# Column-tiled transposes and spreads, and score matmuls of 64 keys, in a transformer block

## The chip, the core and the metric

The kernel runs on one core of a Trainium2 chip. The metric is the device time of one execution in microseconds (us). The engines are PE (TensorE, matmuls; PEld are its weight loads), DVE (VectorE), ACT (ScalarE), POOL (GpSimd) and SP (SyncE, which only issues DMAs here).

## What is computed

One transformer block with conditioned norms, for x of 4 x 1024 x 512, 16 heads of 32 channels, a hidden width of 2048, all in float32:

```python
def _tc_rmsnorm(x, t, gw, gb, bw, bb):
    g = (t @ gw.T + gb)[:, None, :]
    b = (t @ bw.T + bb)[:, None, :]
    inv_rms = jax.lax.rsqrt(jnp.mean(x * x, axis=-1, keepdims=True) + EPS)
    return g * x * inv_rms + b

def _attention(x, Wq, Wk, Wv, Wo):
    ...
    attn = jnp.einsum('blhd,bmhd->bhlm', q, k) / scale
    p = jax.nn.softmax(attn, axis=-1)
    o = jnp.einsum('bhlm,bmhd->blhd', p, v).reshape(B, L, D)
    return o @ Wo.T

def _swiglu(x, gate_w, hid_w, out_w):
    return jax.nn.silu(x @ gate_w.T) * (x @ hid_w.T) @ out_w.T
...
x1 = x + _attention(_tc_rmsnorm(x, t, g1...), Wq, Wk, Wv, Wo)
x2 = x1 + _swiglu(_tc_rmsnorm(x1, t, g2...), gate_w, hid_w, out_w)
return x + x2
```

The softmax subtracts each row's maximum before the exponential.

## The kernel before

**Layout.** Channels lie on the 128 partitions and tokens along the free axis. The tokens come in 8 blocks of 512 (two for each of the 4 batch entries). Heads are taken in 4 groups of `HG` = 4 heads (4 x 32 = 128 channels), queries in runs of `HQ` = 256, keys in units of 256 (`UN` = 4 units for 1024 keys).

**Steps.** One main loop runs over `g`. Step g computes the raw scores of one unit: 4 heads, 256 queries, 256 keys, so there are 256 such steps; four steps (the kinds g mod 4 = 0 to 3, as counted by `kind`) cover one head group and one run of queries, a group of four steps. The later parts of that attention work follow a few steps behind. From `FS` = 60 on, the feed-forward part of an earlier block is woven into the same steps (`pair_15`, `pair_26`, `pair_7`, `pair_3`, `pair_4`, `contract`: the tiles `pa`, `pb` and `pc`); before it, the projections of queries, keys and values (`pkq`, `pv`) are. After the last scores only feed-forward work is left. The order of the instructions on PE, DVE, ACT and POOL is written out by hand in this loop; each engine runs its own list in order and waits on semaphores.

**Tilings of PE's array.** A matmul with weights of K rows and M columns may use a part of the array: with 32 rows and 128 columns four matmuls of different rows can be in the array, with 128 rows and 32 columns four of different columns. `mm` (line 103) cuts a matmul into column pieces of `columns[0]`, which the loop sets to 32 at the top of each step and to 128 for a while in steps of kind 0 before g = 60. So feed-forward and projection blocks are mostly tiled 128x32, as is `weighted` (line 368, tile `av`: the probabilities times the values, one matmul for each key block and head into that head's 32 partitions). Each float32 matmul call becomes two pairs of a weight load and a matmul instruction; a bfloat16 call becomes one pair.

**The parts that the change touches.**

- `scores` (line 301, matmul on line 310, tile `sc`): for each of two blocks of 128 keys and each of the four heads, one matmul whose weights are that head's 32 rows of 128 keys and whose moving operand is that head's 32 rows of 256 queries. 8 calls a step, tiled 32x128. `keep` (line 315) copies `sc` to `raw` on ACT, with one buffer of `sc`.
- `running_max`, `max_T` and `parts` (lines 319 to 342): DVE takes the maximum over the key blocks, PE transposes it (tile `mt`) and DVE writes the negative of the maximum as three bfloat16 numbers that add up to it, for each head, into columns 0 to 11 (`NP` = 12) of `split`. The remaining columns are zeros.
- `parts_T` (line 344, transposes on line 347, tile `pt`): in steps of kind 1, two bfloat16 transposes of the whole 128x128 `split`, and a copy of the first 12 rows to `mT` on ACT (line 349).
- `spread` (line 351, matmul on line 357, tile `sp`): called twice in steps of kind 1, each time for two of the four heads. A matmul of `select` (12 rows, 128 columns of zeros and ones for each head) with `mT` adds the three parts of the head's negative maximum and spreads the sum over all 128 partitions; ACT copies that to `shift` (line 358). 2 calls each time.
- `shifted` (line 360, DVE) adds `shift` to `raw`, `exponential` (line 365, ACT) takes the exponential in place, and `weighted` and `accumulate` (a DMA issued by POOL) use it.

In a step of kind 1 the order on PE is `parts_T`, `scores`, `spread` of the first two heads, `weighted`, `spread` of the other two, and then the feed-forward or projection blocks:

```python
            if kind == 1 and m_on:
                parts_T(j_m)
            if g < NR:
                scores(g)
            if kind == 1 and m_on:
                spread(j_m, 0)
...
            if v_on:
                weighted(r_v)
                accumulate(r_v)
            if kind == 1 and m_on:
                spread(j_m, 2)
```

In the other steps it is `scores`, `weighted`, then the rest. In the feed-forward stage `weighted` and the feed-forward blocks around it are tiled 128x32.

Of the kernel before, what the change touches and what calls it, by code (L numbers as in the profile page):

```python
# [11 lines left out]
BF16 = mybir.dt.bfloat16  # L12
# [5 lines left out]
P = 128  # L18
# [6 lines left out]
def tile_cond_transformer_block(  # L25
# [13 lines left out]
    nc = tc.nc  # L39
# [7 lines left out]
    DH = D // N_HEADS  # L47
    HG = P // DH
    FG = 4
    HQ = 256  # L50
# [6 lines left out]
    const = ctx.enter_context(tc.tile_pool(name="const", bufs=1))  # L57
    sb = ctx.enter_context(tc.tile_pool(name="sb", bufs=1))
# [8 lines left out]
    ident_bf = const.tile([P, P], BF16, tag="ident_bf", name="ident_bf")  # L67
# [8 lines left out]
    NP = 3 * HG  # L76
    split = [const.tile([P, QT, P], BF16, tag=f"split{i}", name=f"split{i}") for i in range(2)]
# [2 lines left out]

    pick = const.tile([NP, HG], F32, tag="pick", name="pick")
    nc.vector.tensor_reduce(pick, ident[:NP, :NP].rearrange("p (h i) -> p h i", i=3), AX.X, ALU.add)
    select = const.tile([NP, HG, P], BF16, tag="select", name="select")
    nc.vector.tensor_copy(select, pick.unsqueeze(2).to_broadcast([NP, HG, P]))
    mod = const.tile([P, 4 * C, B], F32, tag="mod", name="mod")

    condT = const.tile([P, B], F32, tag="condT", name="condT")
# [15 lines left out]
    def mm(dst, w, moving, start: bool, stop: bool, seeded: bool = False):  # L103
        n = columns[0]
        for k in range(0, P, n):
            nc.tensor.matmul(  # L106
                dst[k : k + n, :], w[:, k : k + n], moving, start=start, stop=stop, skip_group_check=seeded
            )

    y, wkq, wv, wo, kq, v = {}, {}, {}, {}, {}, {}  # L110
    raw, rmax, shift, mT, av, acc, avs, oT = {}, {}, {}, {}, {}, {}, {}, {}
# [189 lines left out]
    def scores(r: int):  # L301

        j, u = divmod(r, UN)
        m, qh = divmod(j, NB // HQ)
        keys, queries = kq[m, 0, u], kq[m, 1, qh]
        sc = ps_sc.tile([P, HG, 2, HQ], F32, tag="sc", name=f"sc{r}")
        for k in range(2):
            for i in range(HG):
                rows = slice(i * DH, (i + 1) * DH)
                nc.tensor.matmul(  # L310
                    sc[:, i, k, :], keys[rows, k * P : (k + 1) * P], queries[rows, :], start=True, stop=True
                )
        state["sc", r] = sc

    def keep(r: int):
# [28 lines left out]
    def parts_T(j: int):  # L344
        pt = ps.tile([P, HQ // P, P], BF16, tag="w", name=f"pt{j}")
        for qt in range(HQ // P):
            nc.tensor.transpose(pt[:, qt, :], split[j % 2][:, qt, :], ident_bf)
        mT[j] = sb.tile([NP, HQ], BF16, tag="mT", name=f"mT{j}", bufs=2)
        nc.scalar.copy(mT[j], pt[:NP, :, :].rearrange("p a b -> p (a b)"))

    def spread(j: int, k: int):

        if k == 0:
            shift[j] = sb.tile([P, HG, HQ], F32, tag="shift", name=f"shift{j}")
        pp = ps.tile([P, 2, HQ], F32, tag="w", name=f"sp{j}_{k}")
        for i in range(2):
            nc.tensor.matmul(pp[:, i, :], select[:, k + i, :], mT[j], start=True, stop=True)
        nc.scalar.copy(shift[j][:, k : k + 2, :], pp)  # L358

    def shifted(r: int, heads: slice = slice(0, HG)):  # L360
# [262 lines left out]
    for b in range(1, B):  # L623
        for half in range(QB):
            s = math.ceil((len(queue) + 1) / PACE)
            s4 = s - 4 - (s - 6) % UN
            tag = f"a{b}_{half}"
# [14 lines left out]
    for n in range(NBLK):  # L642
# [7 lines left out]
        if n < NBLK - 1:  # L650
            tag = f"f{n}"
# [46 lines left out]
    with tc.manual_schedule(  # L698
# [69 lines left out]
        while g < END:  # L768
# [10 lines left out]
            p = (g - FS) // 2  # L779
# [3 lines left out]
# [6 lines that stand above are left out]
# [14 lines left out]
            if kind == 1 and m_on:  # L803
                spread(j_m, 2)
                mT.pop(j_m)
                shifted(r_x, slice(0, HG // 2))
                shifted(r_x, slice(HG // 2, HG))
# [196 lines left out]
```

## Time and profile before

| | |
|---|---|
| time, median of 3 runs | 2479.35 us (2477.35 to 2480.38) |
| the profiled execution | 2480.0 us, of which the profile's span 2478.1 us |
| mean granted PE clock | 0.998 |
| score matmuls, line 310 | x4096, 293.3 us busy |
| transposes, line 347 | x128, 17.6 us busy |
| spread matmuls, line 357 | x256, 49.0 us busy |
| feed-forward stage, 535 to 2245 us | PE 1655.16, DVE 1457.81, ACT 1015.73 us busy |

The span runs from the first to the last instruction of the program. An engine's busy time is the union of its instructions; ends of matmuls are modelled, and pipelined matmuls overlap, so the distance between the starts of two blocks tells more of PE's pace than a duration. In lines of the timeline the columns are the start and the busy time in us, the engine, the line of the kernel, the operation, what is written and read, the tiling as rows\*columns of the array, the shape and the count; in brackets stands the idle time of the engine before it and who ended it. Lines of the list of waits read: who waited for whom, us in total, times, the longest. In the view of one line, durations are minimum, median and maximum in ns.

### The profile page before, as it was taken

To read this page: it belongs to the slowest core of one execution; us is meant where nothing else is said; L and a number is where in the kernel's file an instruction comes from. 1 tells how busy PE (TensorE), PEld (TensorE's weight loads), DVE (VectorE), ACT (ScalarE), POOL (GpSimd) and SP (SyncE) were. 2 spreads that over 40 slices of the span, in tenths; PEclk is the share of its full clock that TensorE was granted. 3 is DMA by queue.
4 is the path that set the end of the run, shared out by engine and by line. 5 is a ranking of instruction groups with operands and counts; after the bars stand their busy time and mean duration, and the time that the engine had idled before them with its cause. 6 is when DMAs were issued, how large, how long until landed. Compare 5 with 4: busy or idle time off the path is not lost. (4 is left out here: it accounts for less than half of the span.)

```text
span 2478.1 us, 71138 instructions
## 1 busy us (share of the span) xinstructions
PE 2396.0 (97%) x31785; PEld 1121.8 (45%) x31785; DVE 1943.7 (78%) x2180; ACT 1412.4 (57%) x1495; POOL 172.4 (7%) x207
## 2 busy tenths in 40 slices
PE   8999999999999999999999999999999999999999
PEld 3333333344444444444444444444444444444444
DVE  2688888888789988998899978997899889843332
ACT  3677777766566656665666656665666566512111
POOL 0000000000000000000000000000000000000000
PEclk9999999999999999999999999999999999999999
DMA  6599998989878888888888888788788888853432
GB/s 214 178 299 251 265 259 221 238 201 238 197 193 203 203 218 200 200 211 214 207 197 207 226 191 204 199 226 203 196 201 212 210 197 199 201 159 116 138 134 71
DMA packets 185982, 501.69 MB, mean 202 GB/s; under 512 B 21319, under 2 KB 78663, under 8 KB 158286
## 3 DMA queue, kind: packets, MB, share of 16 engines
q0 software_dynamic: 28656, 208.68, 43.6%
q1 hardware_dynamic: 156734, 288.47, 34.2%
q8 instruction: 250, 4.10, 0.6%
q14 instruction: 54, 0.44, 0.1%
q10 hardware_dynamic: 288, 0.01, 0.0%
HBM read 246.44 MB, written 41.97 MB: 116 GB/s over the span
## 5 line engine op out<-in xcount | busy, mean ns | idle before, releaser
L363 DVE TENSOR_TENSOR raw<-raw,shift 128x2048 f32<-128x2048 f32 (+1 forms) x320 | 593.9, 1859 | 65.2 <-ACT shift L358 62.3
L366 ACT ACTIVATE raw<-raw 128x2048 f32<-128x2048 f32 x256 | 490.8, 1917 | 214.3 <-DVE raw L363 213.8
L317 ACT COPY raw<-sc 128x2048 f32<-128x2048 f32 x256 | 479.6, 1873 | 169.9 <-PE sc L310 129.7
L322 DVE TENSOR_TENSOR rmax<-rmax,raw 128x1024 f32<-128x1024 f32 x384 | 469.5, 1223 | 53.9 <-ACT raw L317 48.2
L106 PE MATMUL pc<-h,ow 128*32 128x512 f32 x4096 | 467.7, 593 | 2.1 <-DMA ow<-in_out_w 1.1
L376 PE MATMUL av<-raw,v 128*32 128x256 f32 x4096 | 274.9, 386 | 50.0 <-ACT raw L366 50.0
L390 POOL DMA_DIRECT2D raw<-raw x192 | 165.3, 861 | 1991.5 <-ACT raw L366 939.1
L310 PE MATMUL sc<-q,k 32*128 32x256 f32 x4096 | 293.3, 400 | 0.2 <-ACT raw L317 0.2
L106 PE MATMUL pa<-x,fa 128*32 128x256 f32 x4096 | 270.0, 381 | 8.8 <-DVE pa L524 8.5
L106 PE MATMUL pa<-sums,fw 128*32 128x256 f32 x4096 | 267.9, 379 | 0.0
L106 PEld LDWEIGHTS pc<-h,ow 128*32 128x32 f32 x4096 | 128.2, 110 | 245.5 <-issue 226.7
L310 PEld LDWEIGHTS sc<-q,k 32*128 32x128 f32 x4096 | 184.9, 184 | 116.5 <-issue 81.5
L106 PE MATMUL pkq<-y,wkq 128*32 128x512 f32 (+1 forms) x1664 | 231.3, 594 | 4.2 <-ACT y L196 4.1
L376 PEld LDWEIGHTS av<-raw,v 128*32 128x32 f32 x4096 | 107.2, 109 | 175.8 <-ACT raw L366 88.0
L106 PEld LDWEIGHTS pa<-x,fa 128*32 128x32 f32 x4096 | 127.6, 110 | 124.7 <-DVE pa L524 30.5
L106 PEld LDWEIGHTS pa<-sums,fw 128*32 128x32 f32 x4096 | 133.2, 110 | 88.2 <-issue 0.5
L539 ACT COPY pb<-pa 128x256 f32<-128x256 f32 x128 | 46.2, 361 | 181.4 <-PE pa L106 180.3
L577 DVE SCALAR_TENSOR_TENSOR res<-pc,res 128x512 f32<-128x512 f32 x128 | 88.2, 689 | 67.2 <-PE pc L106 62.9
L556 ACT ACTIVATE t<-pa 128x512 f32<-128x512 f32 x128 | 78.1, 610 | 109.9 <-PE pa L106 109.5
L106 PE MATMUL pa<-x,fw 128*32 128x256 f32 x2048 | 135.2, 381 | 0.0
L106 PE MATMUL pb<-x,fw 128*32 128x256 f32 x2048 | 134.0, 379 | 1.2 <-ACT pb L539 1.2
L106 PE MATMUL pb<-sums,fa 128*32 128x256 f32 x2048 | 133.9, 379 | 0.0
(106 smaller groups left out, 2152.4 us busy)
## 6 DMA issues: line engine op xcount, KB each, us to landing
raw<-raw POOLq DMA_DIRECT2D x192, 1024.0 KB, 9.1
fw<-sw SPq DMA_DIRECT2D x128, 512.0 KB, 7.0
fa<-in_gh_w SPq DMA_DIRECT2D x128, 384.0 KB, 5.9
ow<-in_out_w SPq DMA_DIRECT2D x128, 256.0 KB, 2.9
wkq<-in_kq_w SPq DMA_DIRECT2D x32, 512.0 KB, 5.9
v<-vs SPq DMA_DIRECT2D x128, 128.0 KB, 5.0
k<-kqs SPq DMA_DIRECT2D x124, 128.0 KB, 7.0
kqs<-st SPq DMA_DIRECT2D x61, 256.0 KB, 7.7
```

Source lines behind the costliest of these rows:

```text
L106: nc.tensor.matmul(dst[k : k + n, :], w[:, k : k + n], moving, start=start, stop=stop, skip_group_check=seeded)
L310: nc.tensor.matmul(sc[:, i, k, :], keys[rows, k * P : (k + 1) * P], queries[rows, :], start=True, stop=True)
L317: nc.scalar.copy(raw[r].rearrange("p k h q -> p h k q"), state.pop(("sc", r)))
L322: nc.vector.tensor_tensor(rmax[j], rmax[j], raw[r][:, k, :, :], ALU.max)
L363: nc.vector.tensor_tensor(t, t, s.unsqueeze(1).to_broadcast(list(t.shape)), ALU.add)
L366: nc.scalar.activation(raw[r], raw[r], AF.Exp)
L376: nc.tensor.matmul(av[j][i * DH : (i + 1) * DH, :], v[m, u][:, k, i * DH : (i + 1) * DH], raw[r][:, k, i, :], start=(kt == 0), stop=(kt == ...
L390: nc.gpsimd.dma_start(out=acc[j].rearrange("p k h q -> p (k h q)"), in_=raw[r].rearrange("p k h q -> p (k h q)"), accum_op=ALU.add,)
L539: nc.scalar.copy(bank_b[p][:, RIGHT], bank_a[p][:, RIGHT])
L556: nc.scalar.activation(state["t", p], bank_a[p], AF.Tanh, scale=0.5)
L577: nc.vector.scalar_tensor_tensor(r, pp, 0.5, r, ALU.mult, ALU.add)
```

## The change

Three edits. `scores` cuts each block of 128 keys into two halves of 64, so that each call has weights of 32 rows and 64 columns and writes 64 partitions: 16 calls a step. `parts_T` transposes only the first 32 columns of `split`, so its weights have 128 rows and 32 columns and it writes 32 partitions. `spread` goes through `mm`, with `columns[0]` at 32 in steps of kind 1, so each call becomes four of 32 columns; its operands now have all 128 rows: `select` and `mT` are filled with zeros below row 12, and `mT` is two fixed tiles that are used in turn, of which the copy on line 349 writes the first 12 rows. The number of instructions on ACT, POOL and SP is unchanged; DVE has three memsets more at the start.

```diff
-    select = const.tile([NP, HG, P], BF16, tag="select", name="select")
-    nc.vector.tensor_copy(select, pick.unsqueeze(2).to_broadcast([NP, HG, P]))
+
+
+    select = const.tile([P, HG, P], BF16, tag="select", name="select")
+    nc.vector.memset(select, 0.0)
+    nc.vector.tensor_copy(select[:NP], pick.unsqueeze(2).to_broadcast([NP, HG, P]))
+    parts_of = [const.tile([P, HQ], BF16, tag=f"mT{i}", name=f"mT{i}") for i in range(2)]
+    for t in parts_of:
+        nc.vector.memset(t, 0.0)
...
-                nc.tensor.matmul(
-                    sc[:, i, k, :], keys[rows, k * P : (k + 1) * P], queries[rows, :], start=True, stop=True
-                )
+                for part in range(0, P, P // 2):
+                    nc.tensor.matmul(
+                        sc[part : part + P // 2, i, k, :],
+                        keys[rows, k * P + part : k * P + part + P // 2],
+                        queries[rows, :],
+                        start=True,
+                        stop=True,
+                    )
...
-            nc.tensor.transpose(pt[:, qt, :], split[j % 2][:, qt, :], ident_bf)
-        mT[j] = sb.tile([NP, HQ], BF16, tag="mT", name=f"mT{j}", bufs=2)
-        nc.scalar.copy(mT[j], pt[:NP, :, :].rearrange("p a b -> p (a b)"))
+            nc.tensor.transpose(pt[:DH, qt, :], split[j % 2][:, qt, :DH], ident_bf)
+        mT[j] = parts_of[j % 2]
+        nc.scalar.copy(mT[j][:NP], pt[:NP, :, :].rearrange("p a b -> p (a b)"))
...
-            nc.tensor.matmul(pp[:, i, :], select[:, k + i, :], mT[j], start=True, stop=True)
+            mm(pp[:, i, :], select[:, k + i, :], mT[j], True, True)
```

## The prediction, as put on record before the change ran

> **What bounds the kernel now.** I began with the busy shares of the page, then the list of what TensorE (PE) waited for, then the timeline of PE in one group of four steps. Words: a step g is one pass of the main loop, a group is four steps (kind = g mod 4), and a round is the set of matmuls, one in each tile of the array, that run side by side.
>
> ```profile
> PE 2396.0 (97%) x31785; PEld 1121.8 (45%) x31785; DVE 1943.7 (78%) x2180; ACT 1412.4 (57%) x1495; POOL 172.4 (7%) x207
> ...
> PEclk9999999999999999999999999999999999999999
> ...
> PE av L376 <- ACT raw L366: 50.0, 61, 2.6
> PE pa L106 <- DVE pa L524: 8.5, 43, 0.2
> ```
>
> PE is busy 97% of the span at a full granted clock, and its largest wait is 50.0 us, in `weighted` for the exponentials. No other engine is above 78%. So time taken out of PE's stream shortens the kernel, except where that wait takes it back. The busy share does not say what PE is busy with; block starts do:
>
> ```profile
> 1215.37 1.05 PE L106 MATMUL pb<-x,fw 128*32 128x256 f32 x16
> 1216.35 1.15 PE L310 MATMUL sc<-q,k 32*128 32x256 f32 x16
> 1217.42 1.07 PE L376 MATMUL av<-raw,v 128*32 128x256 f32 x16
> 1218.31 1.05 PE L106 MATMUL pa<-x,fw 128*32 128x256 f32 x16
> 1219.17 1.05 PE L106 MATMUL pa<-x,fa 128*32 128x256 f32 x16
> ```
>
> Each line is a block of 16 matmul instructions: 8 calls, each run as two. Between blocks of one tiling, 128x32, the step is 0.86 (1218.31 to 1219.17): four rounds of 0.216. Into the scores, tiled 32x128, it is 0.98, out of them 1.07, and the block after takes 0.89. The excesses over 0.864 are 0.11, 0.21 and 0.02. The view of line 310 splits the middle one:
>
> ```profile
> L310 PE MATMUL sc<-q,k x4096: 374/374/478, 50.6 to 2133.9; 32*128 32x256 f32 x196
> ```
>
> The 4 matmuls of the first round record 478 ns, the others 374 (their mean on the page is 400 = (4 x 478 + 12 x 374) / 16). So 0.104 of the 0.21 is the first load of 128 columns, which nothing hides, and about 0.106 is a drain before the next tiling starts. The 0.02 after it is the unhidden load of 32 columns. A change of tiling thus costs a drain of 0.11 plus a first load of 0.02 (32 columns) to 0.10 (128). A step of kind 1 pays it more often:
>
> ```profile
> 1231.38 1.05 PE L106 MATMUL pb<-x,fw 128*32 128x256 f32 x16
> 1232.38 0.27 PE L347 MATMUL pt<-ident_bf,split 128*128 128x128 bf16 x2
> 1232.58 1.15 PE L310 MATMUL sc<-q,k 32*128 32x256 f32 x16
> 1233.55 0.38 PE L357 MATMUL sp<-mT,select 12*128 12x256 bf16 x2
> 1233.85 1.07 PE L376 MATMUL av<-raw,v 128*32 128x256 f32 x16
> 1234.86 0.39 PE L357 MATMUL sp<-mT,select 12*128 12x256 bf16 x2
> 1235.17 1.07 PE L106 MATMUL pa<-x,fw 128*32 128x256 f32 x16
> 1236.06 1.05 PE L106 MATMUL pa<-x,fa 128*32 128x256 f32 x16
> ```
>
> Steps: 1.00, 0.20, 0.97, 0.30, 1.01, 0.31, 0.89. The spread (sp) after the scores starts 0.97 later, which is 0.864 + 0.104 with no drain: 12 rows by 128 columns counts as the scores' tiling, though the type changes. There are five changes here: pb to pt, pt to sc, sp to av, av to sp, sp to pa.
>
> **The change part by part**, per group in the feed-forward stage, from the lines above.
>
> Transposes (L347) in 128x32: pb to pt loses its change, 1.00 - 0.864 = -0.13. The two transposes still run one after the other in one tile, 0.11. pt to sc stays a change.
>
> Scores to spread: now a change, 64-column score tiles to 128x32: +0.11 drain and +0.02 first load = +0.13.
>
> Spread to av: two spread matmuls stream about 0.22 (half an f32 block's round each), so of 0.30 (0.309 before rounding) the drain is 0.09; with the 0.02 load that av no longer exposes, -0.11. The second spread's changes go too: av to sp 1.01 - 0.864 - 0.02 = -0.12 and sp to pa 0.31 - 0.22 + 0.02 = -0.11. Each spread call becomes four, one per 32 columns, side by side like av's four column tiles (0.216 a round), so its stream stays 0.22; rows 12 to 127 are zeros that cost nothing, as stream time goes by columns.
>
> Sum without the scores: -0.13 + 0.13 - 0.11 - 0.12 - 0.11 = -0.34.
>
> Scores: 8 calls become 16, each of 64 columns, so a round has eight tiles. The trace shows no eight at once. It shows four row tiles at once (sc) and four column tiles at once (av), both at 0.216 a round, so two column halves by four row groups could give four rounds again, 0.86. The other end is four at a time: eight rounds, 1.73. I take 0.86, because each kind of splitting alone already shows full overlap. The first load falls between 0.024 (32 columns) and 0.104 (128); for 64 I take 0.051 on the line between them: -0.05. The drain counts from the last tile started: four loads span 0.13 with 110 ns each, so tiles start 6.7 ns apart, and four more add +0.027.
>
> ```profile
> 1218.09 0.13 PEld L106 LDWEIGHTS pa<-x,fw 128*32 128x32 f32 x4
> ```
>
> Net of the scores: -0.026 in every step, between -0.08 (32-column load, no extra drain) and +0.027 (no gain in load).
>
> A rule and a row disagree about these loads. Above, loads for av, all 128 rows of one row group, run under matmuls of the same rows and the rounds stay 0.216. The Trainium skill (TensorE: Matmul & The Clock Gate, Part 3, "What overlaps and what doesn't") says a weight load overlaps matmuls in flight only when the row group differs, which the two halves of a row group do not satisfy. By the rule the other three rounds would each show a 0.05 load: 3 x 0.053 x 256 = an estimated 41 us more; by the row, none. I go by the row. The same page's table has 16 tiles of 32x32 at 10.6 times one, which speaks for eight at once; no run here shows it.
>
> What the gain meets. The kind-1 part, -0.34 - 0.026 = -0.37, lies on PE's own stream: `mT` is copied (361 ns) long before the spread asks, since a whole score block lies between, and there DVE waits for ACT's copy of the spread (62.3 us in all) and that copy for PE (97.8 us). Kind 2 keeps its -0.026. In kinds 3 and 0 the score gain is mostly eaten: `weighted` waits for the exponential in 42 of 49 such groups, on a chain (sub, reciprocal, shift, exponential) that starts at PE's pb of kind 2 and does not get shorter. Six groups also wait in kind 2, for a chain that starts at the second spread and saves only 0.26 of the 0.39: -0.8 us of gain.
>
> Count: the 61st score block (g = 60) starts at 527.6, so 49 of the 64 groups are in the feed-forward stage. 49 x (0.367 + 0.026) = 19.3; + 7 x 0.052 = 0.4; - 0.8. Before g = 60 the transposes follow 128x128 blocks with no change and wait for DVE's split, so that -0.13 is absent: 15 x 0.24 = 3.5, halved to about 2 because DVE and ACT set part of that stage. The setup's extra memsets (DVE idle 9.1 us there) cost nothing. Queues, ACT and POOL keep their instructions. Sum: 21 us. Against the profiled span, 2478.1 - 21 = 2457; the median of the runs is 1.25 above that span, so 2458.
>
> Own range: best, all scores gain 0.08: 49 x 0.50 + 3 = 28, giving 2451. Worst: transposes gain nothing (-0.13 lost) and the drain costs with no gain in load: 49 x (0.183 - 0.027) = 8, giving 2472.
>
> **The rivals.**
> 1. *Slower: the scores run four tiles at a time.* Place: every score block; price +0.864 x 256 = 221 us, of which at most the 50 us of PE's wait could hide some; 2458 + 221 - 25 = about 2650 (2629 to 2679). It decides the sign once a block grows by more than 0.08. For it: no eight-tile round exists in the trace, and two halves of a row group stream the same rows twice. Against: the four column tiles of av also stream the same rows, each for itself, at full rate.
> 2. *Slower, slightly: each round of scores shows its load.* 3 x 0.051 x 256 = 39 us; 2458 + 39 = 2497. For it: 32 loads a block instead of 16. Against: at 6.7 ns a tile, eight take 54 ns of a 216 ns round.
> 3. *No change: the gain is waited away.* DVE is 85% busy in the feed-forward stage (1457.81 of 1710); if the waits of `weighted` grow in every kind-0 step by what kind 1 saves, 49 x 0.35 comes back: 2458 + 17 = 2475. Against: DVE itself waits for PE in that chain (L546, 97.0 us).
> 4. *The tiling does not stay*: bf16 after f32 could drain even in one tiling. Against: sc to sp, above, shows none. Then only 0.05 a step is left; 2472, the worst of my own range.
>
> **How the numbers follow.** Own forecast, fourth rival included: 0.74; rival 1: 0.14; rival 2: 0.06; rival 3: 0.06. A measurement of this kernel tells about 0.2% (5 us) from no change. Faster by that (under 2474.4): 0.73, with 0.01 of the own case lost to no change; same: 0.07; slower: 0.20. The predicted time is that of the likeliest case, 2458. The range runs from 2446, a little below the best of my bounds, to 2498, which takes in rivals 2 and 3 and leaves out rival 1 and little else. The likeliest case alone is 2451 to 2472.
>
> **What would show it.** Right: pb to pt 0.86 and pt to sc unchanged; a score block that steps 0.92 + 0.13 with first-round matmuls about 50 ns longer than the rest; av to sp and sp to pa without excess; sc to sp 0.13 dearer. PE's wait for the exponential grows by 2 to 3 us. Wrong: score blocks of 1.7 us (rival 1), rounds of 0.27 (rival 2), a wait for `raw` grown by 15 us or more (rival 3), or sp to av with a drain left (rival 4). The forecast falls as a whole if PE starts to sit idle before loads with no releaser, since its program grows by 4096 + 768 pairs of load and matmul (31785 now).

## The result, and the profile after

The changed kernel takes 2474.86 us (median of 20 runs, 2473.0 to 2480.36); the kernel before, in 20 runs beside it, 2478.97 us (2476.48 to 2480.38). The ratio is 0.9986, with a 95% interval of 0.9979 to 0.9993. The interval lies below 1, so a gain is there, but it is 4 us, less than the 0.2% (5 us) from which the prediction counts a difference: no change by its mark, where the forecast was 2458 us. The profiled spans are 2478.1 and 2472.7 us.

First, the busy time of PE on the page of the profile after, with the granted clock, to be set beside PE 2396.0 us before:

```profile
PE 2382.6 (96%) x36648; PEld 1098.6 (44%) x36649; DVE 1940.0 (78%) x2183; ACT 1411.7 (57%) x1495; POOL 172.8 (7%) x207
...
PEclk9999999999999999999999999999999999999999
```

PE has 13.4 us less work and the span is only 5.4 us shorter, so PE waits more. The list of PE's waits after (who waits for whom, us, times, longest):

```profile
PE av L387 <- ACT raw L377: 56.7, 64, 2.6
```

Before, it was 50.0 us in 61 waits. Next the timeline of PE after, kind 1 of the same group that the prediction shows (columns: start and duration in us, engine, line, operation, operands, tiling, shape, count):

```profile
1229.41 1.05 PE L112 MATMUL pb<-x,fw 128*32 128x256 f32 x16
1230.41 0.27 PE L358 MATMUL pt<-ident_bf,split 128*32 128x128 bf16 x2
1230.61 1.12 PE L317 MATMUL sc<-q,k 32*64 32x256 f32 x32
1231.66 0.40 PE L112 MATMUL sp<-mT,select 128*32 128x256 bf16 x8
1231.89 1.03 PE L387 MATMUL av<-raw,v 128*32 128x256 f32 x16
1232.81 0.40 PE L112 MATMUL sp<-mT,select 128*32 128x256 bf16 x8
1233.03 1.05 PE L112 MATMUL pa<-x,fw 128*32 128x256 f32 x16
1233.90 1.07 PE L112 MATMUL pa<-x,fa 128*32 128x256 f32 x16
```

The steps are 1.00, 0.20, 1.05, 0.23, 0.92, 0.22, 0.87, where before they were 1.00, 0.20, 0.97, 0.30, 1.01, 0.31, 0.89. Scores to spread became dearer, as forecast; spread to av, av to spread and spread to pa became cheaper. But pb to pt still takes 1.00, although both are now tiled 128x32. From pb to the last pa 4.68 became 4.49.

The scores by themselves, in the view of their line (minimum, median, maximum of a duration in ns) and in the timeline at the place where the prediction shows them:

```profile
L317 PE MATMUL sc<-q,k x8192: 374/374/426, 50.2 to 2129.9; 32*64 32x256 f32 x200
```

```profile
1214.28 1.12 PE L317 MATMUL sc<-q,k 32*64 32x256 f32 x32
1215.32 1.07 PE L387 MATMUL av<-raw,v 128*32 128x256 f32 x16
1216.21 1.05 PE L112 MATMUL pa<-x,fw 128*32 128x256 f32 x16
```

A block has twice the calls and still takes four rounds of 0.216: eight tiles of 32x64 run at once (in the trace the eight matmuls of a round start 6 or 7 ns apart). The first round records 426 ns against 374, so 0.052 of load is shown in place of 0.104 (478 against 374). The step to av is 1.050 in place of 1.076 (from unrounded starts): -0.026.

Where the rest went is seen when one regular group (of the 49 in the feed-forward stage) is laid over the same group before, both counted from the start of pt. Starts in us, worked out from the two traces; the third row is the forecast's, summed from its own terms:

| | sp 1 | av | sp 2 | pa | sc, kind 2 | sc, kind 3 | av, kind 0 | next pt |
|---|---|---|---|---|---|---|---|---|
| before | 1.170 | 1.479 | 2.482 | 2.800 | 6.390 | 14.490 | 21.470 | 30.550 |
| after - before | +0.082 | +0.001 | -0.085 | -0.187 | -0.178 | -0.128 | -0.066 | -0.066 |
| forecast | +0.10 | -0.01 | -0.13 | -0.24 | -0.24 | -0.26 | -0.26 | -0.39 |

PE is 0.18 ahead when kind 1 is over, and 0.066 ahead at the end; over all whole groups of the stage the median gain is 0.06. The loss has places: `weighted` of kind 2 loses 0.05, `weighted` of kind 0 loses 0.09. The latter waits for a row of work on DVE. DVE's row in this group after, from the timeline of DVE (in brackets: idle time before, and who ended it):

```profile
1065.85 2.36 DVE L374 TENSOR_TENSOR raw<-raw,shift 128x1024 f32<-128x1024 f32 x2 [1.17 <-ACT shift L369]
1068.70 2.49 DVE L333 TENSOR_TENSOR rmax<-rmax,raw 128x1024 f32<-128x1024 f32 x2 [0.50 <-ACT raw L328]
1071.11 0.43 DVE L535 TENSOR_TENSOR pa<-pa,p 128x256 f32<-128x256 f32 x1
1071.55 0.69 DVE L572 SCALAR_TENSOR_TENSOR h<-t,pa 128x512 f32<-128x512 f32 x1
1072.34 0.69 DVE L575 TENSOR_TENSOR h<-pb,h 128x512 f32<-128x512 f32 x1
1072.95 2.28 DVE L374 TENSOR_TENSOR raw<-raw,shift 128x2048 f32<-128x2048 f32 x1
1075.14 2.48 DVE L333 TENSOR_TENSOR rmax<-rmax,raw 128x1024 f32<-128x1024 f32 x2
1077.54 0.68 DVE L588 SCALAR_TENSOR_TENSOR res<-pc,res 128x512 f32<-128x512 f32 x1
1078.14 0.42 DVE L557 TENSOR_TENSOR pb<-pb,p 128x256 f32<-128x256 f32 x1
1078.47 1.74 DVE L427 RECIPROCAL total<-total 128x256 f32<-128x256 f32 x1
1080.25 0.43 DVE L436 TENSOR_TENSOR oT<-avs,total 128x256 f32<-128x256 f32 x1
1080.59 2.28 DVE L374 TENSOR_TENSOR raw<-raw,shift 128x2048 f32<-128x2048 f32 x1
```

From 1068.70 on the view shows no gap in this row until `shifted` for kind 0 (1080.59). This is the regular case: in 26 of the 47 whole groups DVE's idle time in this row adds up to less than 0.4 us, in the others to 0.6 us or more. What the row began with is on ACT, and what it ends in is on ACT and PE; timelines of the same group, ACT first:

```profile
1066.31 0.59 ACT L369 COPY shift<-sp 128x512 f32<-128x512 f32 x1 [0.50 <-PE sp L112]
1066.80 1.88 ACT L328 COPY raw<-sc 128x2048 f32<-128x2048 f32 x1
1068.56 0.39 ACT L413 COPY avs<-av 128x256 f32<-128x256 f32 x1
1068.82 1.94 ACT L377 ACTIVATE raw<-raw 128x2048 f32<-128x2048 f32 x1
...
1082.91 1.91 ACT L377 ACTIVATE raw<-raw 128x2048 f32<-128x2048 f32 x1 [1.43 <-DVE raw L374]
```

Then PE, `weighted` of kind 2 and of kind 0:

```profile
1070.81 1.07 PE L387 MATMUL av<-raw,v 128*32 128x256 f32 x16
...
1084.87 1.07 PE L387 MATMUL av<-raw,v 128*32 128x256 f32 x16 [0.42 <-ACT raw L377]
```

and, in the same group of the kernel before, of kind 0:

```profile
1086.81 1.07 PE L376 MATMUL av<-raw,v 128*32 128x256 f32 x16 [0.30 <-ACT raw L366]
```

So the second spread releases ACT's copy (0.59), behind it stands the copy of the scores (1.88), which releases DVE; DVE works without a gap for 14 us, then the exponential, then PE. A shorter row hangs on the same copy: from 1066.31 ACT goes on without a gap over the copy of the scores and the copy of av (0.39) to the exponential that ends at 1070.76, and `weighted` of kind 2 starts at 1070.81. Laid over the kernel before, all of these are early by the same amount: the second shift copy by 0.060, the copy of the scores by 0.060, the exponential of kind 0 by 0.063, `weighted` of kind 0 by 0.066. What PE gains behind the second spread only makes its wait in kind 0 longer (0.30 to 0.42).

### The profile page after: what moved, and what is told of

Same layout as the page of the kernel before. It is cut to its first block, busy times and chain, and to the rows that moved or that the text cites. A ratio compares the mean times of both kernels' runs of the same rounds, so it can differ in the third digit from the quotient of the medians.

```text
span 2472.7 us, 80869 instructions
## 1 busy us (share of the span) xinstructions
PE 2382.6 (96%) x36648; PEld 1098.6 (44%) x36649; DVE 1940.0 (78%) x2183; ACT 1411.7 (57%) x1495; POOL 172.8 (7%) x207
## 5 line engine op out<-in xcount | busy, mean ns | idle before, releaser
L317 PE MATMUL sc<-q,k 32*64 32x256 f32 x8192 | 286.5, 387 | 0.2 <-ACT raw L328 0.2
L317 PEld LDWEIGHTS sc<-q,k 32*64 32x64 f32 x8192 | 151.1, 131 | 130.0 <-issue 83.2
L112 PEld LDWEIGHTS pa<-x,fa 128*32 128x32 f32 x4096 | 122.6, 110 | 131.7 <-DVE pa L535 36.4
```

The lines of the kernel that those rows point to most:

```text
L112: nc.tensor.matmul(dst[k : k + n, :], w[:, k : k + n], moving, start=start, stop=stop, skip_group_check=seeded)
L317: nc.tensor.matmul(sc[part : part + P // 2, i, k, :], keys[rows, k * P + part : k * P + part + P // 2], queries[rows, :], start=True, stop ...
```

## The experiments

Each was timed beside the kernel before, whose medians in the four batches were 2478.28, 2478.79, 2478.39 and 2478.44 us. Where kinds are compared, the time from the start of one block of scores to the next is taken by kind over the feed-forward stage, from the one profiled execution of each kernel. A sum over the stage holds single events of a microsecond or more (between before and after one step of kind 0 differs by 1.74 us, the spell of lower clock that the last section shows), so medians are given beside sums where it matters. The texts on record speak of three theories. *Stream*: what PE saves or loses in its own stream counts, and the difference to the forecast lies in terms within kind 1. *Loop*: the row through ACT and DVE shown above sets the group's length, so that only what lies ahead of the second spread counts. *Two-stretch* (two-halves in the first texts), formed after the first batch: that row sets the time from the second spread to `weighted` of kind 0 (stretch A), and PE sets it from there to the next second spread (stretch B).

**The parts alone (e1, e2).** e1 is the kernel before with the `scores` of the diff alone, e2 the changed kernel with the `scores` of before (these lines the other way round):

```diff
-                nc.tensor.matmul(
-                    sc[:, i, k, :], keys[rows, k * P : (k + 1) * P], queries[rows, :], start=True, stop=True
-                )
+                for part in range(0, P, P // 2):
+                    nc.tensor.matmul(
+                        sc[part : part + P // 2, i, k, :],
...
```

> The kernel before with the 64-key scores alone; transposes and spread stay as before. Loop theory (in the feed-forward stage the length of a group of four steps is set by DVE's unbroken row of work plus a short link over PE and ACT, from DVE's release of the pc bank over transposes, scores and both spreads to ACT's copies; only what brings the second spread nearer to that release counts): the spread after the scores now follows a change of tiling (32x64 to 12x128), so both spreads come 0.10 to 0.12 us later in each of 64 groups, and what scores save in the other steps is waited away: 2 to 8 us slower than before, about 2484. Stream theory (PE's own sum counts): 192 x -0.026 + 64 x 0.10 = +1 us, no change, 2480.

Measured: 2485.49 us (2482.41 to 2486.38), ratio 1.0029 [1.0019, 1.0040]: slower. Kind 1 of e1, timeline of PE:

```profile
1235.08 1.12 PE L311 MATMUL sc<-q,k 32*64 32x256 f32 x32
1236.13 0.39 PE L362 MATMUL sp<-mT,select 12*128 12x256 bf16 x2
1236.44 1.07 PE L381 MATMUL av<-raw,v 128*32 128x256 f32 x16
```

Before, the spread stayed in the scores' tiling and came 0.97 after them; 1.05 now: the cut scores turn that step into a change, and 0.08 to 0.09 ahead of the second spread shows in each group (kind 1 median +0.093, kind 0 +0.052), while the gain in kinds 2 and 3 is 0.027 each.

> The changed kernel with its scores put back to 128 keys; column-tiled transposes and spread stay. Loop theory: the second spread comes 0.06 earlier than before (0.085 in the changed kernel, less 0.03 for the longer first load and the shorter drain): 49 x 0.06 = 3 us faster than before, about 2476. Stream theory: PE's kind-1 stretch is shorter by about 0.15 a group: 64 x 0.15 = 10 us faster, 2469.

Measured: 2479.54 us (2477.93 to 2482.77), ratio 1.0005 [0.9996, 1.0014]: no change. Kind 1 gains 0.150 a group, kind 0 and kind 2 take back 0.064 and 0.050. Neither part gains alone. e1 is what the loop theory said. e2 is 3.5 us above the loop's number and 10 above the stream's, so it speaks against the stream and fits the loop only in that what kind 1 gains is mostly taken back.

**More work for PE, less for DVE (e3, e4).** In kind 0, DVE adds the two halves of the sums of the exponentials (`fold_sum`, 1.22 us) before PE sums over partitions. e3 (on the kernel before) and e4 (on the changed one) leave the fold out and let PE sum both halves:

```diff
-        for i in range(HG):
-            nc.tensor.matmul(total[i * DH : (i + 1) * DH, :], ones_sum, a[:, 0, i, :], start=True, stop=True)
+        for k in range(2):
+            for i in range(HG):
+                nc.tensor.matmul(
+                    total[i * DH : (i + 1) * DH, :], ones_sum, a[:, k, i, :], start=(k == 0), stop=(k == 1)
+                )
...
-            if kind == 0 and n_on:
-                fold_sum(j_n)
```

> The kernel before without DVE's fold of the two halves of the exponentials' sums (1.22 us of DVE a group); PE adds the halves itself, with 4 more matmul calls, 0.43 us a group. Loop theory: DVE's row is shorter by 1.22, so PE's waits for the exponential (40 us in the feed-forward stage) and for pa (8.5) go and PE's 0.43 x 64 = 27 us come in: 10 to 25 us faster than before, about 2460. Stream theory: PE is the bound, so slower by up to 27 us, less whatever of the waits is freed by chance: 2490 to 2506.

> The same edit on the changed kernel. Loop theory: with DVE's row shorter, PE's stream is the bound and the change's gain on PE (0.18 in kind 1 and 0.026 in each other step, more if the wait for the pc bank goes too) shows: 10 to 18 us faster than the kernel before with the same edit, about 2447. Stream theory: it stands to that kernel as the change stands to the kernel before, 4 us faster.

Measured: 2499.44 us (2497.96 to 2499.72), ratio 1.0083 [1.0070, 1.0097], and 2494.55 us (2492.73 to 2500.15), 1.0072 [1.0059, 1.0085]. Both missed the loop theory by far, and both are what the stream theory said (2490 to 2506 us, and the change worth 4 us: 4.9). Kind 0 grew by 0.39 a group (median), of the 0.43 that it grows by in the stage before g = 60, so little came back from DVE. A reading that keeps DVE's row is that the fold lies behind `weighted` of kind 0, where PE leads and DVE follows. That gave the two-stretch theory, which says what to relieve: DVE's row of kinds 1 to 3.

**DVE's row relieved (e5, e6, e9, e10).** e5 and e6 move the reciprocal and the normalization from kind 2 into kind 1, where DVE waits 1.17 us for the shift copy; e9 and e10 move the reciprocal alone, in the feed-forward stage alone. The diff is that of e9 and e10; in e5 and e6 `normalize(j_n)` goes with it and nothing asks for `ffn`:

```diff
+                if ffn and n_on and j_n < direct and j_n % GB != GB - 1:
+                    inverse(j_n)
                 shifted(r_x, slice(0, HG // 2))
...
-                inverse(j_n)
+                if not ffn:
+                    inverse(j_n)
```

> The kernel before with DVE's reciprocal and normalization (1.74 + 0.43 us a group) moved from step kind 2 into the wait that DVE has in kind 1 before the shift. Two-halves theory (a group is a stretch set by DVE, from the second spread and ACT's copy of the scores in kind 1 to the exponential that weighted waits for in kind 0, and a stretch set by PE, from there to the next group's second spread): the first stretch gets 1.4 to 2.2 us shorter, PE's waits for the exponential in kind 0 (28 us in the feed-forward stage) and for pa (8.5) go, PE becomes the bound throughout: 2444 to 2462, about 2452. Stream theory (PE's sum counts already): nothing is taken from PE, so no change, 2475 to 2480.

> The same move in the changed kernel. Two-halves theory: with no DVE stretch left, all of what the change saves on PE counts, 0.18 in kind 1 and 0.026 in each of three other steps, 49 x 0.26 = 13 us in the feed-forward stage and a little before it: 10 to 16 us faster than the kernel before with the same move, about 2439. Stream theory: 4 us faster than that kernel, as the change stands to the kernel before.

Measured: e5 2449.53 us (2448.16 to 2453.88), 0.9886 [0.9872, 0.9899], and e6 2446.95 us (2445.06 to 2450.0), 0.9873 [0.9858, 0.9888]. e5 is what the two-stretch theory said and far from the stream's. e6 missed: it lies 2.6 us below e5, not 13, nearer to the stream theory's 4. With 2.2 us put in, DVE's `shifted` of kind 1 starts later than the shift copy allows, and `weighted` of kind 2 waits for that (it starts 1.39 after its scores in the group above, 1.125 in the changed kernel, 1.050 where nothing is waited for); kind 2 grew by 5.4 us against e5. The next pair therefore moved less.

> The kernel before with only the reciprocal (1.74 us) moved from kind 2 into DVE's wait in kind 1, and only in the feed-forward stage; the normalization stays in kind 2. Two-stretch theory: the gain of the first such move in that stage, about 40 us, stays and its loss before that stage (12 us) goes; the shift in kind 1 is delayed by 0.5 instead of 0.9, so kind 2's weighted waits less: about 2437 (2432 to 2444).

> The same move in the changed kernel. Two-stretch theory: the row of DVE no longer takes back what PE saves; what is left of taking back is kind 2's weighted, which waits for ACT's row (second shift, scores, av, exponential), about 0.07 a group. So 49 x (0.255 - 0.07) = 9 us, and 1 before that stage, faster than the kernel before with the same move, about 2427. Flat theory (the change is worth its 4 us wherever it stands): 2433.

Measured: e9 2432.21 us (2431.38 to 2433.24), 0.9815 [0.9802, 0.9829]; e10 2427.26 us (2424.4 to 2432.68), 0.9798 [0.9784, 0.9811], faster than both kernels of the case. The same row of DVE in e10, same group:

```profile
1050.71 1.74 DVE L427 RECIPROCAL total<-total 128x256 f32<-128x256 f32 x1
1052.37 2.29 DVE L374 TENSOR_TENSOR raw<-raw,shift 128x1024 f32<-128x1024 f32 x2
1054.82 2.49 DVE L333 TENSOR_TENSOR rmax<-rmax,raw 128x1024 f32<-128x1024 f32 x2 [0.16 <-ACT raw L328]
```

and `weighted` of kind 0 in PE's timeline, without a wait:

```profile
1069.44 1.12 PE L317 MATMUL sc<-q,k 32*64 32x256 f32 x32
1070.49 1.07 PE L387 MATMUL av<-raw,v 128*32 128x256 f32 x16
```

One reciprocal of 1.74 us a group, moved out of a stretch that was bound by DVE, was worth 46 us, more than ten times the change: DVE's row does set the length of that stretch. And with it kind 0 takes nothing back: from e9 to e10 (the change alone) kind 1 gains 7.6 us, kind 3 1.3, kind 0 loses 0.25 and kind 2 loses 4.6, where from before to after kind 0 lost 3.3. By medians a group, kind 0 loses 0.089 from before to after and 0.087 from e3 to e4, where DVE's row of kinds 1 to 3 is as it was, and gains 0.026, what the scores save, from e5 to e6 and from e9 to e10, where that row is relieved. The group of the table above shrinks from 29.729 us in e9 to 29.550 in e10, by 0.179, where from before to after it shrank by 0.066; over the 47 whole groups the medians are 0.121 and 0.058.

The times do not show this. The change is worth 4.1 us from before to after, 4.9 from e3 to e4, 2.6 from e5 to e6 and 4.9 from e9 to e10, where the two-stretch theory said 10 for the last: half came, and a change worth its 4 us everywhere fits as well. That e10 met its 2427 is luck, since e9 came out 5 us below its own forecast of 2437. The runs of e10 spread over 8 us and the profiled one is the slowest; up to its last block of scores it is 6.0 us ahead of e9 (after stands 3.9 ahead of before there), and behind that block it loses 5.4.

**The order on DVE (e7, e8).** The tile pt lies in a PSUM buffer (PSUM is the memory that PE's results go to) of the pool that also holds pc, and DVE's `res<-pc`, which empties pc, ends 0.05 before pt starts. In the changed kernel:

```profile
1093.21 0.69 DVE L588 SCALAR_TENSOR_TENSOR res<-pc,res 128x512 f32<-128x512 f32 x1
...
1093.95 0.27 PE L358 MATMUL pt<-ident_bf,split 128*32 128x128 bf16 x2
```

In 48 of the 50 steps of the stage that hold a pt the trace names this eviction as its releaser. e7 puts that eviction ahead of the `running_max` of kind 0; e8 adds the move of e6:

```diff
+                if kind == 0:
+                    evict()
                 if g < NR:
...
-                if evict is not None:
+                if kind != 0:
                     evict()
```

> The changed kernel with DVE's release of the pc bank put ahead of the running maximum in kind 0. The transposes start 0.348 us after the last round of pb; the lone change of tiling that they had is gone (0.240 where no pc comes before), so the rest is the wait for that bank. If so: 0.108 a group comes off PE's stretch, 47 x 0.108 = 5 us faster than the changed kernel, about 2470. If the 0.348 is a drain that the transposes need whatever their columns: no change, 2475.

> Both moves in the changed kernel. Two-halves theory: about 5 us below the changed kernel with the reciprocal moved, 2434. Stream theory: 2470.

Measured: e7 2475.39 us (2472.66 to 2479.34), 0.9989 [0.9981, 0.9998], the changed kernel's time; e8 2464.69 us (2461.65 to 2471.62), 0.9946 [0.9932, 0.9959], slower than e6. Both missed. DVE's timeline of e7 says why:

```profile
1062.72 0.69 DVE L588 SCALAR_TENSOR_TENSOR res<-pc,res 128x512 f32<-128x512 f32 x1 [1.53 <-PE pc L112]
1063.33 1.22 DVE L336 TENSOR_TENSOR rmax<-raw 128x1024 f32<-128x1024 f32 x1
```

The eviction starts when pc ends, in either order. With the maximum behind it, DVE first idles 1.53 and is then late for kind 1, which shows in no time of e7 and costs kind 2 dearly in e8 (36 us more in kind 2 than before). So e7 did not take the wait away, and it cannot tell a wait for the bank from a drain.

**Another bank for the transposes (e11, e12, e15).** The transposes become matmuls with the identity into the free half of av's PSUM bank (the buffer that `weighted` sums into), so that they wait for no eviction of pc; e11 on the changed kernel, e12 and e15 on e10, e15 with `start=False`:

```diff
+            half = next(iter(av.values()))[:, HQ:]
+            for qt in range(HQ // P):
+                nc.tensor.matmul(
+                    half[:DH, qt * P : (qt + 1) * P],
+                    split[j % 2][:, qt, :DH],
+                    ident_bf,
+                    start=True,
...
-            av[j] = ps_av.tile([P, HQ], F32, tag="av", name=f"av{j}")
+            av[j] = ps_av.tile([P, NB], F32, tag="av", name=f"av{j}")
```

With `start=True` in e11 and e12 the output has a relative error of 0.27; e15, which differs from e12 in this flag alone, keeps the sums. So the flag that begins a sum acts on the other half of the bank too, most likely on the first head's values, whose partitions the transposes write.

> The changed kernel with the transposes written, as plain matmuls with the identity in float32, into the free half of the bank of av instead of the bank that pc has just used. Bank theory: their 0.348 after the last round of pb is DVE's eviction of pc (res), not a drain; it falls to 0.24, the second spread comes 0.108 earlier in 47 groups, and that counts, since it is ahead of the second spread: 5 us faster than the changed kernel, about 2470. Drain theory (transposes drain PE's array whatever their columns and bank): no change, 2475.

> Both moves in the changed kernel. Two-stretch and bank theory together: 5 us below the changed kernel with the reciprocal moved, about 2422. Drain theory: as that kernel, 2427.

> The changed kernel with the reciprocal moved, and the transposes as fp32-output matmuls into the free half of av's bank, without the start flag, so that they leave the sums of the first head alone. If the gain of the same kernel with the start flag (2424) came from the wait for the bank that is gone, the flag makes no difference: 2422 to 2426. If the flag mattered for the time: 2427 (no gain).

Measured: e11 2470.03 us (2466.88 to 2471.39), 0.9966 [0.9952, 0.9979]; e12 2424.34 us (2419.41 to 2427.36), 0.9781 [0.9768, 0.9795]; e15 2423.53 us (2418.64 to 2428.02), 0.9777 [0.9761, 0.9793]. Timeline of PE in e15:

```profile
1045.11 1.05 PE L112 MATMUL pb<-x,fw 128*32 128x256 f32 x16
1045.97 0.28 PE L359 MATMUL av<-ident_bf,split 128*32 128x128 bf16 x2
```

pb to pt is 0.86, four bare rounds, in all 50 such steps of e11 and of e15: without the wait for the bank, no change of tiling is left here. (These are plain matmuls and not transposes; the two groups of the changed kernel without a pc ahead keep the transposes, and there the step after the last round is 0.240, 0.024 above a bare round.) Kind 0, which ends with this step, is 7.0 us shorter in e12 and 7.6 in e15 than in e10 (49 x 0.13 = 6.4; the median of a group is 0.128). The 0.13 of the forecast was real and lay under another wait. By time, every run of e11 lies below every run of the changed kernel; e12 and e15 have the lowest medians of the study, 2.9 and 3.7 us below e10, but their runs overlap with e10's, so there the time alone decides nothing.

**ACT's row (e13, e14, e16).** What took back 4.6 us in kind 2 of e10 could be ACT's row from the second shift copy to the exponential of kind 2, in which the copy of av stands (0.39). e13 (on e9), e14 (on e10) and e16 (on e15) give that copy to DVE in the feed-forward stage:

```diff
-        nc.scalar.copy(avs[j], av.pop(j))
+        (nc.vector.tensor_copy if on_dve else nc.scalar.copy)(avs[j], av.pop(j))
```

> The kernel before with the reciprocal moved to kind 1 in the feed-forward stage (2432 us), and there too the copy of av in kind 1 taken from ACT to DVE (0.39 us of ACT per group, between the second shift copy and the exponential of kind 2). ACT-row theory: in this kernel weighted of kind 2 waits little, so 2430 to 2434, no change. If ACT's row bounds kind 2 here too: 2427 or less. DVE theory (DVE's row of kind 1 is what the shift of kind 2 waits for, as in the kernels with more work moved to kind 1): slower, 2437 or more.

> The same on the changed kernel with the reciprocal moved (2427 us). ACT-row theory: the wait of weighted in kind 2, which took back 4.6 us of the 9.5 that kinds 1 and 3 gained, goes, so 2423 to 2424 and kind 2 back to the ticks of the same kernel on before. DVE theory: the wait in kind 2 stays or grows, 2428 or more.

> Both of the last two together. ACT-row theory: each of the two waits is in another step, so the gains add: 2420 (2418 to 2422). If both remove the same wait: 2423 to 2424.

Measured: e13 2435.1 us (2431.07 to 2438.54), 0.9820 [0.9807, 0.9833]; e14 2428.64 us (2425.1 to 2430.73), 0.9796 [0.9783, 0.9810]; e16 2428.39 us (2421.81 to 2432.49), 0.9794 [0.9778, 0.9810]. By the time, no gain; a miss for e14 and e16, and e14 lies where the DVE theory put it (2428 or more). By the steps, ACT's row was the place: in e14 kind 2 takes about 8.07 us in 28 of the 49 groups, in e10 in 6 (8.15 in most others), and its sum falls by 3.1 us, of which 1.0 is a single step. But the list of PE's waits in e14 has a new line:

```profile
PE pmf L112 <- DVE avs L413: 5.4, 6, 0.9
```

DVE comes to the copy 0.9 us late in the six groups in which a norm's matmul stands behind it, and kind 1 pays 4.0 us. One wait went and another came, and e16 has the same wait with 6.2 us. The runs of e10 and e14 overlap, so which is faster stays open.

## Why the prediction was wrong

- *Scores, -0.026 a step; eight tiles at once*: right, to the digit (0.864 + 0.104 + 0.106 became 1.050). Rivals 1 and 2 fell with it. The Trainium skill's rule (TensorE: Matmul & The Clock Gate, Part 3, "What overlaps and what doesn't") that a load overlaps only matmuls of other row groups is not what the trace shows: both halves of each row group run in one round of 0.216, and only the first round shows a load.
- *Scores to spread, +0.13*: +0.08 measured. *Spread to av, -0.11*: -0.08. The forecast's +0.10 to the first spread and -0.01 to av were +0.082 and +0.001: two errors that cancel by luck.
- *av to spread, -0.12*, and *spread to pa, -0.11*: -0.086 and -0.102. The second spread waits for ACT's first shift copy, whose PSUM buffer it takes, and starts 0.051 after that copy ends; the block after next starts 0.052 after the second copy ends, and it and the one behind it are together 0.031 late against bare rounds. The forecast took ACT's copies as far away on the strength of `mT`, and did not ask for those of the spreads.
- *pb to pt, -0.13*: 0 measured. The step between the starts was read as a drain. It was the wait for DVE's eviction of pc, with the drain hidden under it; e11 and e15 show it. In the two groups with no pc ahead the step after the last round did fall, from 0.331 to 0.240. The bound "transposes gain nothing" stood in the range, not in the value taken.
- *Transposes to scores* stayed a change (0.203 and 0.202), and rival 4 fell: bfloat16 after float32 in one tiling drains nothing (0.86 from pb to pt in e15), nor does float32 after bfloat16 (0.23 from spread to av, 0.01 above its two rounds).
- *What the gain meets* is the step that failed. It held that kind 1's part lies on PE's own stream and counted 0.367 a group in full, with 0.026 for kind 2. It let the chain that `weighted` of kind 0 waits for start at PE's pb of kind 2. That block comes 0.129 earlier in the changed kernel, and the chain only 0.06 earlier: DVE is busy without a gap from further back, and its row is released by the second spread through ACT's copies. Of the 0.393 a group, 0.128 went to the bank, 0.059 mostly to ACT's copies within kind 1 (0.237 forecast behind pt, 0.178 found), 0.076 to the wait in kind 2 (from -0.178 to -0.128, where another -0.026 was forecast) and 0.062 to the one in kind 0 (from -0.128 to -0.066, where nothing was). What is left is 0.066, or 3.2 us in 49 groups, of 19.3.
- *Rival 3* is the mechanism of the last two, and its price of 2475 is the measured time, though it had one of the two smallest shares of the chances. The price is met in part by luck: it let kind 0 take back all that kind 1 saves, and a good part had been lost before, at the bank and the copies. The argument against it, that DVE waits for PE in that chain (97.0 us), was read from a sum over the whole kernel: 79.1 of the 97.0 us lie behind the last block of scores, and from kind 1 to kind 0 DVE's row has no gap in the regular group.
- *What is shown.* For the wait of kind 0, e9 and e10 show the cause by the steps, since with one reciprocal moved out of DVE's row kind 0 no longer takes anything back; the time of that pair does not (4.9 us, about what the change is worth without the move). Kind 2 still took back 0.05 a group. That this is ACT's row is shown by its timeline above and by the steps of e14, not by a time.
- *The stage before g = 60, 2 us*: 1.4 measured. The feed-forward stage gave 2.1 of the 5.4 us by which the spans differ; the remaining 1.9 lie ahead of the first block of scores and behind the last.

## What to carry to other kernels

A PE that is busy 97% of the span can still follow another engine: take one period, follow each engine's row of work back to its last gap, find the instruction that ended that gap, and count a saving in full only if it lies ahead of that instruction. A step between two starts is a sum of causes that hide each other, so before a drain or a load is taken as saved, look for the buffer that the second block writes and for who empties it. A sum of waits over the whole kernel does not say in which stage they lie. A direct test is to relieve the other row: here one reciprocal, moved into an idle stretch, was worth more than ten times the change.

## What the runs showed of the hardware

- Sixteen float32 calls of 32x64 take four rounds of 0.216, as eight of 32x128 do. The load shown by the first round goes by columns: 0.024 for 32, 0.052 for 64, 0.104 for 128.
- PE's clock fell to half once behind a short idle time. In the changed kernel PE waited 1.62 us at 1018.8, and the view of stretches (us; PE, PEld, DVE, ACT, POOL busy; clock; DMA share, GB/s) shows:

```profile
1018.00:1022.00 4.00, 2.18 (x56) 0.95 (x44) 4.00 (x6) 3.52 (x5) 0.58 (x1) 1.00 0.85 217
1022.00:1026.00 4.00, 4.00 (x43) 1.91 (x36) 3.58 (x3) 2.35 (x4) 0.28 (x1) 0.57 1.00 254
```

A clock of 0.57 over 4 us is about 3.4 us at half speed. The other waits of 1.62 us in this trace had no such sequel. The Trainium skill (TensorE: Matmul & The Clock Gate, Part 1, "What's actually happening") gives a window of 3.4 us and an idle window as the cause. The length agrees; an idle time of that length did not precede this spell. That the 1.62 us caused it is not shown.
- The last DMA that adds exponentials lands at varying times. At the end of the attention PE waits for it through DVE, 4.20 us in the profile of e10 and 0.25 in e15's, and around the long wait the clock falls (0.69 from 2143 to 2150 us, 0.79 to 2156), around the short one it does not (1.00); the four runs of e10 lie at 2424.4, 2424.7, 2429.8 and 2432.7. Differences of 3 us between such medians are no finding.
